# An empty VectorE instruction for the waits of a state-space scan, and TensorE sums of two units at a time

## The chip, the cores and the metric

The kernel runs on one core of one Trainium2 chip. The metric is the device time of one execution in microseconds (us). The engines named below are TensorE (PE in the profile, PEld for its weight loads), VectorE (DVE), ScalarE (ACT), GpSimd (POOL) and SyncE (SP, which issues most DMAs). Each engine works through its own instructions in order; between engines, and between an instruction and an earlier one of its own engine, order is kept by semaphores that an instruction waits for. A name such as DVEq is the instruction queue of that engine: a wait that is an instruction by itself is shown there as EVENT_SEMAPHORE.

## The reference

Two transformer-like layers on x of shape (4, 256, 512). Layer 0 is a latent attention plus a gated feed-forward part. Layer 1 adds a selective state-space block and a mixture of low-rank experts. All of the change lies in the state-space block, for each of the four batches with d = 1024 channels, n = 16 states and 256 time steps:

```python
xc = silu(causal_conv4(x) + conv_b)                # (d, t)
ssm_p = xc projected to 32 + 16 + 16               # dt_r, Bm, Cm, each rms-normed
dt = softplus(dt_r @ dt_proj + dt_bias)            # (d, t)
# scan over t, for each channel d and state n:
h = exp(dt_t * A) * h + dt_t * B_t * x_t
y = sum_n h * C_t
out = ((ys + D * xc) * silu(z)) @ out_proj
```

## The kernel before

Layer 0 comes first (up to about 330 us, with its last matmuls, L469, to 350 us). Then the scan runs through 128 units. Unit u works on batch b = u // 32 (a pass), on a chunk c = u % 32 // 4 of 128 channels, and on a group g = u % 4 of 4 states. A unit's tile has 128 partitions and 4 x 256 elements: partitions hold 32 channels for each of 4 states, and the free dimension holds 4 blocks of 32 channels by 256 time steps. The steps of a unit:

- `decays(u)` on ScalarE: four activations (L980) write the decay exp(dt * A) into one of three rotating tiles `decay`. A tile can be written again when the scan of three units before has read it.
- `scan_in(u)` on VectorE: the input product `bx` = B * (dt * x) (L986), from PSUM `brow` and the spread tile `dus`, into one PSUM tile of its own. As there is one such tile, the product waits for the scan of the unit before, which reads it.
- `scan(u)` on VectorE: one scan instruction over all 1024 elements (L1001), `h` = decay * h + bx. `h` has two buffers, so the scan must wait until the product of `h` and C of two units before has been made.
- the same function then makes `hc` = h * C on GpSimd (L1006; the last quarter of the last unit on VectorE). `hc` has three buffers.
- `states_sum(u)` on TensorE: four matmuls with a stacking matrix (L1018) add the 4 states into one quarter each of the PSUM tile `ysum`, as matmuls 32 columns wide. Each is traced as two, so that one unit has 8. In the first unit of a chunk (g = 0) a full-width matmul (L1016) opens the sum with D * xc; it waits until the sum of the chunk before has been copied out.
- After the fourth unit of a chunk, `take_sum` on ScalarE (L1023) copies the sum to `xc`, and `gate` on GpSimd (L1026) multiplies it by silu(z).

The order on every engine is written out by hand: the schedule is manual, and each engine executes its instructions in the order in which the main loop issues them. In iteration u the loop issues, in this order: `take_sum` where a chunk ended two units before; `decays(u + 2)`; the side work that is put at u (dictionary `at`); `scan_in(u)`; work put in the middle (`mid_at`); `scan(u)`; `gate`; late work; `states_sum(u - 1)`; work put at the end (`end_at`).

The side work prepares the next batch during the present pass. By its place in a pass of 32 units: norm and projection `px` (L757), convolution as matmuls (L804) with taps from ScalarE (L774, L779, L785) and additions on GpSimd (L811), in units 0 to 16; the silu of all of `xc` on ScalarE (L820, with a change of its function table) at unit 16; the projection `pp` (L831) in two halves, the first at the very end of unit 17, the second at 18; its squares and their mean (L837, L838) at 19; `nrm` on VectorE (L845) between product and scan of unit 21; then step sizes on TensorE (L870), ScalarE (L875 to L887) and GpSimd (L914 to L918, and `du`, L925), in units 21 to 30. `dt` and `du` go through DRAM (dtd, dud) and come back spread over the partitions (`dts`, `dus`) by DMAs from SP (L939). The experts' routing (L1053 to L1085) takes some 20 small VectorE instructions at unit 25 of passes 0 and 2. The output matmuls (L1114), the gate's input `pz` (L948) and the dense part (L1105) fill in.

A VectorE instruction carries one wait by itself; further ones stand in separate wait instructions in front of it, with up to two waits each. So before a scan there is one wait instruction, for the product and the decay, and the scan itself carries the wait for GpSimd.

Of the kernel before, what the change touches and what calls it, by code (L numbers as in the profile page):

```python
# [11 lines left out]
AF = mybir.ActivationFunctionType  # L12
# [16 lines left out]
NG = 4  # L29
# [12 lines left out]
def block_kernel(  # L42
# [24 lines left out]
    nc = tc.nc  # L67
# [51 lines left out]
    live = {}  # L119
# [363 lines left out]
    def go(gen, n=1000):  # L483
        for _ in range(n):
            if next(gen, 1) == 1:
                break
# [169 lines left out]
    xcs, nrms, dts, szs, crows = {}, {}, {}, {}, {}  # L656
# [15 lines left out]
    aneg = w1.tile([P, DC, NG, NU], F32, name="aneg")  # L672
# [15 lines left out]
        pads.append(t)  # L688

    decay = []  # L690

    def decay_tile(pool):
        t = pool.tile([P, NG, S], F32, name=f"decay{len(decay)}")
        nc.gpsimd.memset(t[:, :, 0:1], 0.0)
        decay.append(t)
# [268 lines left out]
    def lend(n, u):  # L964
        tag = lent[n][u]
        pool, bufs = (we, 3) if tag == "w_in" else (w1, 1)
        return pool.tile([P, NG, S], F32, tag=tag, name=n, bufs=bufs)

    def decays(u):
        b, c, g = u // PER, u % PER // NU, u % NU  # L970
        if u >= len(lent["d"]):
            da = decay[(u - 4) % 3]
        elif lent["d"][u] == "d":
            da = decay[0]
        else:
            da = lend("d", u)
            nc.gpsimd.memset(da[:, :, 0:1], 0.0)
        live["da", u] = da
        for k in range(NG):
            nc.scalar.activation(da[:, k, 1:], live["dts", b, c][:, k, 1:], AF.Exp,  # L980
                                 scale=aneg[:, c, k, g : g + 1])

    def scan_in(u):
        b, c, g = u // PER, u % PER // NU, u % NU
        bx = psx.tile([P, NG, S], F32, tag="bx", name="bx")
        nc.vector.tensor_tensor(  # L986
            bx, brow[g // 2][:, g % 2, :].unsqueeze(1).to_broadcast([P, NG, S]), live["dus", b, c], ALU.mult
        )
        live["bx"] = bx

    def scan(u, parts=1):
        b, c, g = u // PER, u % PER // NU, u % NU
        da, bx = live.pop(("da", u)), live["bx"]
        if u < len(lent["h"]):
            h, hc = lend("h", u), lend("hc", u)
        else:
            h = act.tile([P, NG, S], F32, tag="h", name="h", bufs=2)
            hc = act.tile([P, NG, S], F32, tag="hc", name="hc", bufs=3)
        for k in range(parts):
            n = slice(k * NG // parts, (k + 1) * NG // parts)  # L1000
            nc.vector.tensor_tensor_scan(  # L1001
                h[:, n].rearrange("p n t -> p (n t)"), da[:, n].rearrange("p n t -> p (n t)"),
                bx[:, n].rearrange("p n t -> p (n t)"), 0.0, ALU.mult, ALU.add,
            )

            (nc.vector if k == NG - 1 else nc.gpsimd).tensor_tensor(  # L1006
                hc[:, n], h[:, n],
                crows[b][:, g, :].unsqueeze(1).to_broadcast([P, NG // parts, S]), ALU.mult,
            )
        live["hc", u] = hc  # L1010

    def states_sum(u):
        b, c, g = u // PER, u % PER // NU, u % NU
        hc = live.pop(("hc", u))
        if g == 0:
            mm(ysum, lhsT=dgs[:, c, :], rhs=xcs[b][:, c, :], start=True, stop=False)  # L1016
        for k in range(NG):
            mm(ysum[k * NB : (k + 1) * NB, :], lhsT=stack, rhs=hc[:, k, :],  # L1018
               start=False, stop=(g == NU - 1))

    def take_sum(b, c):

        (nc.scalar.copy if b or c else nc.vector.tensor_copy)(xcs[b][:, c, :], ysum)  # L1023

    def gate(b, c):
        nc.gpsimd.tensor_tensor(  # L1026
            xcs[b][:, c, :], xcs[b][:, c, :], szs[b, c // 2][:, c % 2, :], ALU.mult
        )
# [84 lines left out]
    def out_mm(b, i, c):  # L1113
        mm(live["po", b, i], lhsT=xcs[b][:, c, i * P : (i + 1) * P], rhs=late_w["ow"][:, c, :],  # L1114
           start=False, stop=(c == DC - 1))
# [33 lines left out]
    for i in range(2):  # L1149
        v = vec[:, 6 + i, :]  # L1150
        nc.scalar.activation(px[:, i, :], px[:, i, :], AF.Identity, bias=v[:, V_CB : V_CB + 1],
                             scale=v[:, V_CW + KC - 1 : V_CW + KC])
# [33 lines left out]
    u, e, lw = live["u"], live["e"], live["lw"]  # L1186
# [21 lines left out]
    for n, t in (("dt", dt[:, 1, :]), ("du", du[:, 1, :])):  # L1208
        live[n, 0, 0] = scr.tile([2, P, S], F32, tag=n, name=f"{n}d")
        nc.sync.dma_start(live[n, 0, 0][1], t)  # L1210
    decays(0)
    scan_in(0)
    spread("dt", 0, 1)
    spread("du", 0, 1)
    b_rows(0, 1)
    c_rows(0, 1)
    decays(1)
    one_step(2)

    def open_act():  # L1220
        nonlocal act
        l0.close()
        act = ctx.enter_context(tc.tile_pool(name="act", bufs=1))
        decay_tile(act)
        decay_tile(act)
        for n, shape, d in (("rl", [P, HC, NE + P], rl_d), ("bw", [P, HC, D], base_d),
                            ("lb", [P, D], lb_d), ("ow", [P, DC, D], ow_d)):
            late_w[n] = act.tile(shape, F32, name=n), d
# [146 lines left out]
    total = B * PER  # L1375
    late, gated = [], []
    for u in range(total + 2):

        last = u - 2
        shut = (last // PER, last % PER // NU) if last >= 0 and last % NU == NU - 1 else None  # L1380
        if shut and shut != (0, 0) and u < total:
            take_sum(*shut)
        if 3 <= u < total - 2:
            decays(u + 2)
        for f, a in at.get(u, ()):
            f(*a)
        if u < total:
            if u:
                scan_in(u)
            for f, a in mid_at.get(u, ()):  # L1390
                f(*a)
        if shut == (0, 0):
            take_sum(0, 0)
        if u > total:
            b, c = shut
            for i in range(2):
                w = slice(i * P, (i + 1) * P)
                nc.vector.tensor_tensor(xcs[b][:, c, w], ysum[:, w], szs[b, c // 2][:, c % 2, w], ALU.mult)
        if u < total:
            scan(u, 1 if u < total - 1 else 4)  # L1400
            if u < 3:
                decays(u + 2)

        for g in range(2):
            o = u - NU - 1 - g
            if u < total and o >= 0 and o % NU == 0 and (o >= total - PER) == (g == 0):
                gate(o // PER, o % PER // NU)
                if g == 0:
                    gated.append(o % PER // NU)
        for f, a in late_at.get(u, ()):  # L1410
            f(*a)
        if 1 <= u <= total:
            states_sum(u - 1)
        if late and u >= total - PER + 22:
            c = late.pop(0)
            for i in range(2):
                out_mm(B - 1, i, c)
        for f, a in end_at.get(u, ()):
            f(*a)
        late, gated = late + gated, []  # L1420
        if u < 3:
            go(ff, (9, 12, 100)[u])
        if u == 2:
            open_act()
# [106 lines left out]
```

## Time and profile before

| | us |
|---|---|
| three timed runs | 839.10, 839.61, 840.86 |
| median of the runs | 839.61 |
| span of the profiled execution | 839.1 |
| VectorE busy | 655.1 (78%) |
| TensorE busy | 748.8 (89%) |
| ScalarE busy | 554.7 (66%) |
| GpSimd busy | 496.7 (59%) |
| products L986, 128 of 1.232 | 157.7 |
| scans L1001, 129 of 2.236 in the mean | 288.2 |
| hc L1006, 130 of 2.323 in the mean | 301.7 |
| sums L1018, 1024 traced matmuls | 89.6 |

The profiled execution has no time of its own beside its span; the span of 839.1 us equals the fastest of the three timed runs. A digit line of the page cuts the span into 40 slices, with the busy share in tenths. A timeline line has start, duration, engine, line, operation, written tile <- read tiles with their shapes, the number of merged instructions, and in brackets the idle time in front with what ended it. A table of busy times by stretch has, after the stretch and its length, the busy time (and instructions) of PE, PEld, DVE, ACT and POOL, the TensorE clock that was granted, the DMA share and GB/s.

### The profile page before, as it was taken

The numbers are of one execution on the slowest core, as the hardware profiler recorded it, in microseconds if no ns is written. First come the engines' busy times: TensorE is split into PE (matmuls) and PEld (weight loads), VectorE is DVE, ScalarE is ACT, GpSimd is POOL, SyncE is SP. The second block draws the span as 40 slices with busy tenths as digits, with TensorE's granted clock in tenths as the row PEclk, the third lists the DMA queues.
The fourth block names the chain that finished last, engine by engine and source line by source line (L and its number), as shares of the span: only waits on it lengthen the run. The fifth ranks groups of instructions, "written<-read, shape, count | busy, mean of one in ns | idle before, by whom it ended". The sixth has DMA issues, their size and how long they took to land.

```text
span 839.1 us, 11113 instructions
## 1 busy us (share of the span) xinstructions
PE 748.8 (89%) x3846; PEld 429.7 (51%) x3846; DVE 655.1 (78%) x604; ACT 554.7 (66%) x1124; POOL 496.7 (59%) x389
## 2 busy tenths in 40 slices
PE   4999999999999999999887899888999987956885
PEld 2665545666555676666543457444457444312331
DVE  4486756288634435798899999989999989999996
ACT  4335564435556277699896898687898786865561
POOL 3133332001343333688869799769699769798764
PEclk9799999999999999999999999989999989998998
DMA  7233332001222332554593554443553343343400
GB/s 226 63 101 105 97 101 62 1 1 38 76 76 80 114 57 64 151 140 125 137 215 114 150 155 125 110 103 117 144 164 114 88 113 111 103 125 102 113 26 25
DMA packets 68642, 86.71 MB, mean 103 GB/s; under 512 B 12221, under 2 KB 52169, under 8 KB 68458
## 3 DMA queue, kind: packets, MB, share of 16 engines
q1 hardware_dynamic: 58794, 65.81, 29.3%
q0 software_dynamic: 9072, 18.35, 7.9%
q10 hardware_dynamic: 720, 1.84, 0.6%
q8 instruction: 30, 0.49, 0.2%
q14 instruction: 26, 0.21, 0.1%
HBM read 66.58 MB, written 10.22 MB: 92 GB/s over the span
## 4 chain that ended last, share of the span: by engine, by line
PE 51%; DVE 25%; ACT 15%; POOL 5%; issue 3%; DMA 1%; DVEq 0%; POOLq 0%; ACTq 0%; SPq 0%
DVE h L1001 15%; ACT decay L980 7%; PE pg L444 6%; PE pu L444 5%; PE po L469 5%; PE px L757 4%; DVE bx L986 4%; POOL hc L1006 4%; PE av L397 4%; PE px L804 4%; PE ysum L1018 3%; PE scT L386 2%; DVE mpl L354 2%; PE pp L831 2%; PE po L1114 2%
## 5 line engine op out<-in xcount | busy, mean ns | idle before, releaser
L1006 POOL TENSOR_TENSOR hc<-h,cr 128x1024 f32<-128x1024 f32 (+1 forms) x130 | 301.7, 2323 | 79.9 <-DVE h L1001 67.5
L1001 DVE TENSOR_TENSOR_SCAN h<-decay,bx 128x1024 f32<-128x1024 f32 (+1 forms) x129 | 288.2, 2236 | 27.0 <-POOL hc L1006 4.7
L980 ACT ACTIVATE decay<-dts,aneg 128x255 f32<-128x255 f32 x504 | 213.4, 501 | 52.3 <-DVE h L1001 42.2
L986 DVE TENSOR_TENSOR bx<-brow,dus 128x1024 f32<-128x1024 f32 x128 | 157.7, 1232 | 5.0 <-DMA dus<-dud 0.6
L1018 PE MATMUL ysum<-hc,stack 128*32 128x256 f32 x1024 | 89.6, 419 | 42.2 <-POOL hc L1006 41.9
L456 POOL TENSOR_TENSOR hlo<-g,hhi 128x512 fp32r<-128x512 f32 x28 | 35.8, 1280 | 115.0 <-ACT hhi L455 115.0
L354 DVE TENSOR_REDUCE mpl<-sc 128x4 f32<-128x1024 f32 x64 | 76.7, 1219 | 22.8 <-PE sc L352 21.3
L427 POOL DMA_DIRECT2D wgu<-in_wgu x56 | 31.1, 555 | 95.9 <-PE pg L444 94.7
L388 ACT ACTIVATE pe<-scT 128x1024 f32<-128x1024 f32 x64 | 64.0, 1023 | 22.9 <-PE sc L352 14.3
L1114 PE MATMUL po<-ow,xc 128*128 128x512 f32 x128 | 69.4, 646 | 4.3 <-POOL xc L1026 3.9
L1018 PEld LDWEIGHTS ysum<-hc,stack 128*32 128x32 f32 x1024 | 21.3, 111 | 100.3 <-POOL hc L1006 70.6
L948 PE MATMUL pz<-xn1T,w_in 128*128 128x256 f32 x256 | 69.4, 420 | 0.0
L948 PEld LDWEIGHTS pz<-xn1T,w_in 128*128 128x128 f32 x256 | 50.8, 208 | 20.7 <-issue 11.9
L757 PE MATMUL px<-xn1T,w_in 128*128 128x256 f32 x256 | 60.9, 383 | 0.4 <-ACT sz L954 0.3
L757 PEld LDWEIGHTS px<-xn1T,w_in 128*128 128x128 f32 x256 | 47.6, 190 | 13.0 <-issue 2.5
L452 DVE SCALAR_TENSOR_TENSOR g<-g,pg 128x512 f32<-128x512 f32 x28 | 19.2, 686 | 43.1 <-ACT g L451 43.1
L444 PE MATMUL pg<-xhi,wgu 128*128 128x512 f32 x112 | 49.6, 443 | 1.0 <-ACT xhi L244 1.0
L469 PE MATMUL po<-wd,hhi 128*128 128x512 f32 x112 | 49.2, 439 | 0.0
L444 PE MATMUL pu<-xhi,wgu 128*128 128x512 f32 x112 | 47.6, 425 | 0.8 <-DVE g L454 0.8
L455 ACT CAST hhi<-g 128x512 fp32r<-128x512 f32 x28 | 17.3, 619 | 45.8 <-DVE g L454 45.8
L444 PE MATMUL pg<-xlo,wgu 128*128 128x512 f32 x112 | 44.9, 401 | 0.7 <-DVE xlo L251 0.7
L444 PE MATMUL pu<-xlo,wgu 128*128 128x512 f32 x112 | 44.5, 397 | 0.0
(237 smaller groups left out, 1276.8 us busy)
## 6 DMA issues: line engine op xcount, KB each, us to landing
dts<-dtd SPq DMA_DIRECT2D x124, 128.0 KB, 2.8
dus<-dud SPq DMA_DIRECT2D x124, 128.0 KB, 3.2
wgu<-in_wgu POOLq DMA_DIRECT2D x56, 256.0 KB, 2.7
w_in<-in_inz SPq DMA_DIRECT2D x16, 512.0 KB, 4.9
w_in<-in_inx SPq DMA_DIRECT2D x14, 512.0 KB, 4.3
dtd<-dt SPq DMA_DIRECT2D x15, 256.0 KB, 2.2
dud<-du SPq DMA_DIRECT2D x15, 256.0 KB, 2.2
wd<-in_wd POOLq DMA_DIRECT2D x7, 512.0 KB, 3.6
```

Source lines behind the costliest of these rows:

```text
L354: nc.vector.tensor_reduce(mpl2[b % 2][:, qb, 2 * hp : 2 * hp + 2, 16 + 2 * gq : 18 + 2 * gq], sc.rearrange("p i (f k) -> p i f k", f=2), A ...
L388: nc.scalar.activation(pes[b, k][:, 2 * t : 2 * t + 2, :], sc, AF.Exp)
L444: mm(ps, lhsT=wgus[i][:, hc, :], rhs=xs[j][:, hc, :], start=(hc == 0 and j == 0), stop=(hc == HC - 1 and j == 1))
L469: mm(po, lhsT=hids[th][j][:, m, i * P : (i + 1) * P], rhs=wd[:, m, :], start=False, stop=(m == MC - 1 and j == 1))
L757: mm(px[:, i, :], lhsT=w[:, i, hc, :], rhs=xns[b][:, hc, :], start=(hc == 0), stop=(hc == HC - 1))
L948: mm(pz[:, i, :], lhsT=w[:, i, hc, :], rhs=xns[b][:, hc, :], start=(hc == 0), stop=(hc == HC - 1))
L980: nc.scalar.activation(da[:, k, 1:], live["dts", b, c][:, k, 1:], AF.Exp, scale=aneg[:, c, k, g : g + 1])
L986: nc.vector.tensor_tensor(bx, brow[g // 2][:, g % 2, :].unsqueeze(1).to_broadcast([P, NG, S]), live["dus", b, c], ALU.mult)
L1001: nc.vector.tensor_tensor_scan(h[:, n].rearrange("p n t -> p (n t)"), da[:, n].rearrange("p n t -> p (n t)"), bx[:, n].rearrange("p n t -> ...
L1006: (nc.vector if k == NG - 1 else nc.gpsimd).tensor_tensor(hc[:, n], h[:, n], crows[b][:, g, :].unsqueeze(1).to_broadcast([P, NG // parts, ...
L1018: mm(ysum[k * NB : (k + 1) * NB, :], lhsT=stack, rhs=hc[:, k, :], start=False, stop=(g == NU - 1))
L1114: mm(live["po", b, i], lhsT=xcs[b][:, c, i * P : (i + 1) * P], rhs=late_w["ow"][:, c, :], start=False, stop=(c == DC - 1))
```

## The change

From unit 8 on, `scan_in` issues an empty VectorE instruction ahead of the product, and two dependencies are added to it by hand: on the last activation of the unit's own decay, and on the `hc` of two units before. As VectorE is in order, both hold for the scan too, so its own waits for ScalarE and GpSimd are left out when waits are assigned, and the scan keeps the one for the product. And `states_sum` is issued in even iterations only, for the units u - 2 and u - 1 one after the other.

```diff
+    made = {}
+    early = mybir.DependencyInfo(mybir.DependencyClass.Sync, mybir.DependencyReason.DATA)
...
         for k in range(NG):
-            nc.scalar.activation(da[:, k, 1:], live["dts", b, c][:, k, 1:], AF.Exp,
-                                 scale=aneg[:, c, k, g : g + 1])
+            made["da", u] = nc.scalar.activation(
+                da[:, k, 1:], live["dts", b, c][:, k, 1:], AF.Exp, scale=aneg[:, c, k, g : g + 1]
+            )
 
     def scan_in(u):
         b, c, g = u // PER, u % PER // NU, u % NU
+        if u >= 8:
+            i = nc.vector.engine_nop()
+            for n in (("da", u), ("hc", u - 2)):
+                tc.add_manual_dep(i.ins, made[n].ins.name, early, reason="the scan's waits")
         bx = psx.tile([P, NG, S], F32, tag="bx", name="bx")
...
-            (nc.vector if k == NG - 1 else nc.gpsimd).tensor_tensor(
+            made["hc", u] = (nc.vector if k == NG - 1 else nc.gpsimd).tensor_tensor(
                 hc[:, n], h[:, n],
...
-        if 1 <= u <= total:
+        if u and u % 2 == 0:
+            states_sum(u - 2)
             states_sum(u - 1)
```

In the built program VectorE has 120 empty instructions (L989) more, 116 of them with a wait instruction in front (for ScalarE), and 120 wait instructions less in front of the scans (12 for 132). The empty instruction itself carries the wait for GpSimd. The order of TensorE's matmuls changes by the sums alone. On SP, the first load of `w_in` for the gate waits for another buffer. On ScalarE and GpSimd the order stays; the first activation of many decays, and many hc's, get one more wait, for earlier work of their own engine.

## The prediction

> **What bounds the kernel now.** I read the digits of the page first, then a table of busy times for the four passes of the scan, then the timelines.
>
> ```profile
> PE   4999999999999999999887899888999987956885
> DVE  4486756288634435798899999989999989999996
> ACT  4335564435556277699896898687898786865561
> ```
>
> Up to 330 us TensorE is full, and the change touches none of that. From there VectorE is, and three others are close behind it. By pass (start:end, length, then PE, PEld, DVE, ACT, POOL busy):
>
> ```profile
> 364.40:465.60 101.20, 86.15 (x484) 53.91 (x483) 90.49 (x75) 86.12 (x195) 85.02 (x53) 0.95 0.60 152
> 465.60:588.70 123.10, 112.48 (x556) 61.32 (x554) 114.58 (x71) 102.41 (x232) 104.06 (x63) 0.92 0.46 124
> 588.70:712.80 124.10, 114.13 (x595) 63.97 (x595) 117.14 (x89) 102.03 (x234) 103.13 (x61) 0.95 0.44 121
> 712.80:828.40 115.60, 85.29 (x416) 33.50 (x415) 110.31 (x63) 71.62 (x153) 90.01 (x50) 0.94 0.31 86
> ```
>
> The last pass is VectorE's alone (110.3 of 115.6 us). In passes 0 to 2 ScalarE, GpSimd and TensorE have bursts that VectorE must wait for. VectorE's timeline shows a calm stretch, the burst of pass 0, and the stall of pass 1:
>
> ```profile
> ...
> 403.26 2.29 DVE L1001 TENSOR_TENSOR_SCAN h<-decay,bx 128x1024 f32<-128x1024 f32 x1 [0.69 <-POOL hc L1006]
> ...
> 419.37 0.48 DVE L845 SCALAR_TENSOR_TENSOR nrm<-pp,lnw,rs 64x256 f32<-64x256 f32 x1 [0.24 <-ACT rs L713]
> 419.77 2.27 DVE L1001 TENSOR_TENSOR_SCAN h<-decay,bx 128x1024 f32<-128x1024 f32 x1
> ...
> 545.65 0.48 DVE L845 SCALAR_TENSOR_TENSOR nrm<-pp,lnw,rs 64x256 f32<-64x256 f32 x1 [1.32 <-ACT rs L713]
> ...
> 603.53 1.23 DVE L986 TENSOR_TENSOR bx<-brow,dus 128x1024 f32<-128x1024 f32 x1
> 604.89 2.29 DVE L1001 TENSOR_TENSOR_SCAN h<-decay,bx 128x1024 f32<-128x1024 f32 x1
> 607.22 1.23 DVE L986 TENSOR_TENSOR bx<-brow,dus 128x1024 f32<-128x1024 f32 x1
> 608.58 2.29 DVE L1001 TENSOR_TENSOR_SCAN h<-decay,bx 128x1024 f32<-128x1024 f32 x1
> ```
>
> A unit takes 3.69 us: product 1.23, a gap of 0.13 (603.53 + 1.23 to 604.89), scan 2.29, a gap of 0.04. The gaps differ because the product waits for one thing, the scan before it, while the scan waits for three (product, decay, GpSimd's hc of two units before) and has a wait instruction of its own ahead of it, which takes 50 ns and cannot end before the product has. In pass 3:
>
> ```profile
> L1001 DVEq EVENT_SEMAPHORE  x31: 50/50/50, 714.1 to 824.7; - x31
> ```
>
> **The change, part by part.**
>
> *The gap.* In units 8 to 127 decay and hc are now waited for by an empty instruction (L989) ahead of the product, and the scan waits for the product alone, as the product waits for the scan. So its gap should be that of the product, 0.04 for 0.13. Rounded less, the two gaps are 132 and 35 ns: 120 units x 0.097 = 11.6 us. This is the whole gain if VectorE is never held by others.
>
> *The empty instruction.* Before has none on VectorE. The waits in front of the product (for dus, every fourth unit) begin as soon as the scan before has begun, and with them the product's gap stays 0.04; so the new wait for ScalarE should hide under the 2.29 us scan. The instruction itself I count as one that the engine executes. Below nothing is excluded: the product still waits for the scan's end. Above, I bound it by the shortest VectorE row, a memset of 128x1 (L87), 0.06 us; three of them start 0.03 apart. VectorE instructions without a wait begin 0.08 us before the one in front ends, so 0.06 fits in front of the scan's end. I take 0, and keep 120 x 0.06 = 7.1 us.
>
> [...]
>
> *What is queued behind the earlier waits.* Where decay or hc is late, the product now stands behind it too and 1.27 us (product and gap) that ran beside the lateness follow it. VectorE is in order, so `nrm` at units 21, 53 and 85, on which the next batch's steps depend, is held too. The hc of two units back normally ends 1.2 us before the product could start, so nothing is exposed; decay mostly ends earlier still. By unit, subtracting the ends in the traces: late ScalarE at 10 (0.7), 20, 51 (0.7), 58, 70 (0.7), 83 (0.4); late GpSimd at 13 to 19 (up to 4.4), 29 to 32 (0.6 falling), 43 to 48 (0.2), 61 to 64 (0.8 falling), 75 to 80 (0.2), 93 to 96 (0.6 falling). In pass 3 nothing.
>
> *The sums in pairs.* TensorE's timeline:
>
> ```profile
> 353.23 1.07 PE L1018 MATMUL ysum<-hc,stack 128*32 128x256 f32 x16
> 354.23 1.13 PE L870 MATMUL pdt<-nrm,dtw 32*128 32x256 f32 x4
> ...
> 411.88 5.35 PE L831 MATMUL pp<-xc,xpw 128*64 128x256 f32 x16 [3.91 <-ACT xc L820]
> 417.17 0.64 PE L1018 MATMUL ysum<-hc,stack 128*32 128x256 f32 x8
> ...
> 499.75 0.64 PE L1018 MATMUL ysum<-hc,stack 128*32 128x256 f32 x8
> 500.32 2.00 PE L804 MATMUL px<-pad,dg 128*128 128x256 f32 x8
> ...
> 534.82 0.70 PE L1016 MATMUL ysum<-xc,dgs 128*128 128x256 f32 x2 [3.07 <-ACT xc L1023]
> ```
>
> One sum takes 0.57 to the next start and 0.2 more at its borders with matmuls of another shape. Two in a row (353.23) take 1.00 and the same borders. A pair saves about 0.34. In the stretch 480 to 528, where TensorE never waited for a sum, 7 pairs give 2.4 us. And the matmul that opens a chunk (L1016) moves half the time a unit later: at 534.82 TensorE stood 3.07 us behind ScalarE's copy of the last chunk, with the projection `pp` (L831) queued behind; now `pp` goes first. So `pp` and `nrm` of pass 1 come several us earlier, and the 1.32 us stall at 545.65 goes. Pass 2 gains less there (0.66 of stall at 657.66).
>
> *The ring of three hc buffers.* The first sum of a pair now stands one slot later, so hc of unit u+3 may find its buffer unread. After unit 16 this bites: its sum, at 407.33 before, falls behind both halves of `pp`, which wait for ScalarE until 411.88 and end at 417.2. GpSimd's hc of unit 19 reads:
>
> ```profile
> 413.26 2.34 POOL L1006 TENSOR_TENSOR hc<-h,cr 128x1024 f32<-128x1024 f32 x1
> ```
>
> It would start at about 418.5 (417.2 + L1016 0.5 + sum 0.6 + 0.2) and end at 420.9. Unit 21's product waits for it: product to 422.1, `nrm` 0.5, scan at 422.65 instead of 419.77, +2.9 us. At unit 48 and 80 the earlier `pp` covers it.
>
> *Other queues.* SP: the first weight load of in_inz waits for a scan at 344.6 us instead of a sum at 336.3; behind it stand dtd, dud and the first spreads. Its matmuls ran at 349.68; a load takes 4.9 us, so 0 to 0.5 us, beside 0.3 saved by the first pair: taken as nothing. ScalarE and GpSimd get one more wait in about half the decays and hc's, on their own finished work: nothing while they are behind, 0.05 us when they wait for VectorE, which is not on the path then.
>
> *The sum* (position against before). Pass 0: +1.3 through the GpSimd burst (units 13 to 19), +2.9 at unit 21, replacing it, -1.0 over the ten units to 31, +1.0 at unit 29: +2.9. Pass 1: -1.9 over 19 units, -1.3 for the stall at `nrm`: -0.3; four units -0.4; units 58 to 61 about -0.1, since ScalarE's chain is two us earlier but the product is exposed; -0.3: -0.8 at 588.7. Pass 2: -3.1, ScalarE at 70 +0.9, GpSimd at 93 +0.8, small ones +0.3: -1.9. Pass 3: 32 x 0.097 = -3.1. Together -5.0. The profiled execution spans 839.1 us, 0.5 below the median of the runs, 839.61; I take the difference from the median: **834.6 us**.
>
> **The rivals.**
>
> *The empty instruction costs its place (slower).* If it starts only after the scan has ended and the product after it, a unit pays 0.06 (the memset) to 0.10 (a wait instruction and its hand-over). At 0.06: 834.6 + 7.1 = 841.7; it decides from 42 ns (5.0 / 120). For it: that a wait instruction on this queue costs 0.1. Against: short instructions start 0.03 apart, and next ones start before the end of the last. 0.2.
>
> *The hc ring or the early waits bite in every pass.* If passes 1 and 2 lose like pass 0 (2.9 each, ScalarE's bursts not coming earlier), 834.6 + 5.8 = 840.4, no change. For it: three passes with the same order around `pp`. Against: the 3.07 us stall that goes. 0.15.
>
> *The bursts move with VectorE.* If ScalarE's and GpSimd's work starts as much earlier as VectorE runs, nothing is exposed: 839.61 - 11.6 = 828.0, or 826.7 with the `nrm` stall. Against: ScalarE has no idle time from 367 to 403. 0.15.
>
> **How the numbers follow.** My forecast has 0.5. About 0.2% (1.7 us) is what can be told from no change. Faster: the forecast nearly whole (0.47) and the third rival (0.15): 0.62. The second rival gives most of "same", 0.12 with the forecast's edge; the first, and the second's bad half, 0.26 slower. The low end, 828.5, takes most of the third rival; the high end, 842.0, the first with its bound. The forecast's own range is 832 to 837.
>
> **What would show it.** Pass 3: units of 3.59 us with both gaps 0.04 (right), or 3.65 and more with a gap after the scan (first rival). Pass 0: hc of unit 19 released by the sum. Pass 1: no stall before `nrm`, L1016 behind `pp`. VectorE's idle time should read "POOL hc" and "ACT decay" in front of the product instead of the scan. It is wrong if pass 3 isn't about 3 us shorter, or if passes 0 to 2 lose more than pass 3 gains.

## The result, and the profile after

| | us |
|---|---|
| before, median of 22 runs | 839.38 |
| after, median of 22 runs | 840.49 |
| ratio after / before, 95% interval | 1.0015 [1.0007, 1.0023] |
| span of the profiled execution, before / after | 839.1 / 840.1 |

In this set the change makes the kernel slower by 0.15%. A second set of runs of the same program gave 840.69 us, where before took 840.81 (ratio 0.9995 [0.9982, 1.0009]), so no clear difference is left. I had forecast 834.6 us, a clear gain. The time lies in the range given, but the gain did not come. A run's time is about 1.8 us longer than the span of its core (841.86 for 840.1 in the profile after), so the profile of before, with 839.1, belongs to a run of about 840.9, the slowest of the three listed and not the fastest; the forecast, a difference taken from the median, does not hang on that.

The digits of the page after:

```profile
PE   4999999999999999989796989988899997976885
DVE  4486755288734435887789999998999999999997
ACT  4335564435556276689886788877898786865661
```

Up to the 17th slice VectorE's digits are nearly those of before. The next four, which hold most of pass 0, read 8 7 7 8 for 9 8 8 9: VectorE waits more there. In the rest, 9s stand for 8s in two slices, and an 8 for a 9 in one. The four passes in the profile after, read as before from the product of unit 8 on (start:end, length, busy PE, PEld, DVE, ACT, POOL, granted clock, DMA share, GB/s):

```profile
364.05:471.61 107.56, 90.23 (x504) 59.17 (x496) 90.41 (x75) 86.12 (x195) 85.44 (x53) 0.92 0.60 146
471.61:594.05 122.44, 108.87 (x564) 62.17 (x564) 114.44 (x71) 102.36 (x232) 104.31 (x63) 0.93 0.46 125
594.05:716.38 122.33, 109.85 (x590) 65.83 (x589) 117.09 (x88) 101.64 (x234) 102.75 (x62) 0.94 0.43 122
716.38:829.40 113.02, 86.46 (x414) 36.83 (x414) 110.30 (x63) 71.25 (x153) 89.56 (x49) 0.88 0.32 87
```

VectorE's busy time is that of before in every pass (90.4, 114.4, 117.1, 110.3 for 90.5, 114.6, 117.1, 110.3). Pass 0 is 6.4 us longer, the others 0.7, 1.8 and 2.6 shorter. So the gain of the gap is there, and something else takes it away. VectorE's timeline after shows both:

```profile
...
549.58 0.47 DVE L847 SCALAR_TENSOR_TENSOR nrm<-pp,lnw,rs 64x256 f32<-64x256 f32 x1
549.98 2.27 DVE L1008 TENSOR_TENSOR_SCAN h<-decay,bx 128x1024 f32<-128x1024 f32 x1
...
564.34 1.23 DVE L993 TENSOR_TENSOR bx<-brow,dus 128x1024 f32<-128x1024 f32 x1 [1.33 <-POOL hc L1013]
565.61 2.29 DVE L1008 TENSOR_TENSOR_SCAN h<-decay,bx 128x1024 f32<-128x1024 f32 x1
570.05 1.23 DVE L993 TENSOR_TENSOR bx<-brow,dus 128x1024 f32<-128x1024 f32 x1 [2.16 <-ACT decay L982]
...
581.60 1.23 DVE L993 TENSOR_TENSOR bx<-brow,dus 128x1024 f32<-128x1024 f32 x1 [0.83 <-POOL hc L1013]
...
608.47 1.23 DVE L993 TENSOR_TENSOR bx<-brow,dus 128x1024 f32<-128x1024 f32 x1
609.74 2.29 DVE L1008 TENSOR_TENSOR_SCAN h<-decay,bx 128x1024 f32<-128x1024 f32 x1
612.06 1.23 DVE L993 TENSOR_TENSOR bx<-brow,dus 128x1024 f32<-128x1024 f32 x1
```

Calm units take 3.59 us with both gaps at 0.035 (608.47 + 1.23 to 609.74, and 609.74 + 2.29 to 612.06). The stall in front of `nrm` in pass 1 is gone. But units 57, 58 and 61 stand in front of their product for 1.33, 2.16 and 0.83 us, and the product runs only when the wait is over. In the groups this is the idle time that moved from the scan (27.0 us before) to the product (5.0 before):

```profile
L1008 DVE TENSOR_TENSOR_SCAN h<-decay,bx 128x1024 f32<-128x1024 f32 (+1 forms) x129 | 288.1, 2236 | 8.1 <-PE po L469 3.2
...
L993 DVE TENSOR_TENSOR bx<-brow,dus 128x1024 f32<-128x1024 f32 x128 | 157.6, 1232 | 27.8 <-POOL hc L1013 12.0
```

Before, 1.23 us of product lay beside each such wait; after, they follow it. The instructions that do the waiting take 13 and 21 ns in the median, and the calm gaps are 0.035 us with them (count, durations min/median/max in ns, first and last start):

```profile
L989 DVEq ENGINE_NOP  x120: 5/13/15, 363.9 to 828.0; - x120
L989 DVEq EVENT_SEMAPHORE  x116: 21/21/21, 363.2 to 825.8; - x116
```

TensorE's timeline at the turn from convolution to projection in pass 1 is as forecast, L1023 (the L1016 of before) now behind both halves of `pp`:

```profile
537.33 1.94 PE L833 MATMUL pp<-xc,xpw 128*64 128x256 f32 x8 [1.24 <-ACT xc L822]
...
540.25 1.94 PE L833 MATMUL pp<-xc,xpw 128*64 128x256 f32 x8
542.12 0.70 PE L1023 MATMUL ysum<-xc,dgs 128*128 128x256 f32 x2
```

GpSimd's timeline in pass 0 has four waits for a sum (in front of hc of units 7, 9, 11 and 19), where before has none. The longest are 3.39 us in front of hc of unit 9 and 5.86 us in front of those of units 19 and 20:

```profile
374.76 2.36 POOL L1013 TENSOR_TENSOR hc<-h,cr 128x1024 f32<-128x1024 f32 x1 [3.39 <-PE ysum L1025]
...
422.22 4.67 POOL L1013 TENSOR_TENSOR hc<-h,cr 128x1024 f32<-128x1024 f32 x2 [5.86 <-PE ysum L1025]
```

It happens in pass 1 as well. hc of unit 55 waits 2.91 us for a sum and ends at 564.30, and this is what unit 57's product waits for, which starts at 564.34:

```profile
561.93 2.37 POOL L1013 TENSOR_TENSOR hc<-h,cr 128x1024 f32<-128x1024 f32 x1 [2.91 <-PE ysum L1025]
```

### The profile page after: what moved, and what is told of

Its sections match the earlier page's. It is cut to its first block, busy times and chain, and to the rows that moved or that the text cites. A ratio compares the mean times of both kernels' runs of the same rounds, so it can differ in the third digit from the quotient of the medians.

```text
span 840.1 us, 11287 instructions
## 1 busy us (share of the span) xinstructions
PE 743.8 (89%) x3846; PEld 439.8 (52%) x3846; DVE 655.1 (78%) x604; ACT 553.9 (66%) x1124; POOL 496.5 (59%) x389
## 3 DMA queue, kind: packets, MB, share of 16 engines
q10 hardware_dynamic: 720, 1.84, 0.6%
## 4 chain that ended last, share of the span: by engine, by line
PE 47%; DVE 26%; ACT 12%; POOL 8%; issue 4%; DMA 2%; SPq 0%; ACTq 0%; DVEq 0%; POOLq 0%
DVE h L1008 12%; DVE bx L993 7%; PE pg L444 6%; POOL hc L1013 6%; PE pu L444 5%; PE po L469 5%; PE av L397 4%; PE px L759 4%; ACT decay L982 3%; PE scT L386 2%; PE px L806 2%; PE ysum L1025 2%; DVE mpl L354 2%; PE po L1121 2%; PE po L464 2%
## 5 line engine op out<-in xcount | busy, mean ns | idle before, releaser
L993 DVE TENSOR_TENSOR bx<-brow,dus 128x1024 f32<-128x1024 f32 x128 | 157.6, 1232 | 27.8 <-POOL hc L1013 12.0
L1025 PE MATMUL ysum<-hc,stack 128*32 128x256 f32 x1024 | 80.6, 416 | 41.6 <-POOL hc L1013 41.6
L1025 PEld LDWEIGHTS ysum<-hc,stack 128*32 128x32 f32 x1024 | 25.4, 113 | 90.1 <-POOL hc L1013 62.4
```

What stands on the lines that cost most here:

```text
L993: nc.vector.tensor_tensor(bx, brow[g // 2][:, g % 2, :].unsqueeze(1).to_broadcast([P, NG, S]), live["dus", b, c], ALU.mult)
```

## The experiments

For each kernel the table has the median, its ratio to before on the same chip with the 95% interval, and from the profile what each pass loses (+) or gains (-). For that I take the start of a scan less its start in the profile of before, set to zero at unit 1, since layer 0, which nothing here touches, differs by up to 2 us between profiles. The passes are read at units 32, 64, 96 and 127.

| kernel | us | ratio | pass 0 | 1 | 2 | 3 | sum |
|---|---|---|---|---|---|---|---|
| changed | 840.49 | 1.0015 [1.0007, 1.0023] | +5.9 | -0.7 | -1.8 | -2.6 | +0.9 |
| changed_again | 840.69 | 0.9995 [0.9982, 1.0009] | +5.8 | -0.6 | -1.7 | -2.6 | +1.0 |
| single_sums | 840.71 | 1.0010 [0.9995, 1.0025] | +0.7 | +1.6 | -0.6 | -2.6 | -0.9 |
| pairs_only | 840.04 | 1.0001 [0.9986, 1.0016] | +4.0 | -3.0 | -1.1 | 0.0 | -0.1 |
| empty_no_waits | 840.01 | 1.0001 [0.9986, 1.0016] | -0.3 | -0.3 | 0.0 | +0.4 | -0.2 |
| pairs_from_32 | 835.02 | 0.9929 [0.9910, 0.9949] | +3.4 | -2.2 | -0.6 | -1.6 | -1.0 |
| pairs_32_again | 834.71 | 0.9943 [0.9930, 0.9956] | +0.7 | -3.2 | -0.8 | -2.6 | -5.9 |
| pairs_32_no_empty | 835.34 | 0.9931 [0.9913, 0.9948] | 0.0 | -3.0 | -1.1 | 0.0 | -4.1 |
| pairs_32_empty_96 | 833.78 | 0.9913 [0.9890, 0.9936] | 0.0 | -3.0 | -0.8 | -2.6 | -6.4 |
| pairs_32_empty_calm | 833.17 | 0.9905 [0.9884, 0.9926] | -0.4 | -1.9 | -1.9 | -2.9 | -7.0 |
| empty_behind | 831.27 | 0.9887 [0.9864, 0.9909] | +3.5 | -5.6 | -4.0 | -3.0 | -9.1 |
| behind_pairs_32 | 826.02 | 0.9834 [0.9810, 0.9858] | -1.3 | -6.4 | -2.8 | -3.0 | -13.5 |
| single_behind | 833.98 | 0.9934 [0.9917, 0.9950] | -1.4 | -0.4 | -1.7 | -2.5 | -6.0 |
| sum16_single | 837.93 | 0.9975 [0.9961, 0.9988] | +4.6 | -1.3 | -1.7 | -2.6 | -1.0 |
| first_sums_single | 840.62 | 1.0003 [0.9990, 1.0016] | +5.5 | -0.5 | -1.7 | -2.6 | +0.8 |
| pairs_from_12 | 838.98 | 0.9992 [0.9980, 1.0004] | +5.2 | -2.5 | -1.6 | -2.6 | -1.4 |
| hc_in_front | 841.06 | 1.0007 [0.9993, 1.0020] | 0.0 | +0.8 | +0.7 | -0.9 | +0.5 |

The profile of pairs_from_32 is of its slowest execution, 838.17 us; the five others took 832.81 to 835.40. The reason comes below.

### The two parts apart

Theory A blamed the pairs in pass 0, theory B the early waits.

single_sums, against the changed kernel:

```diff
-        if u and u % 2 == 0:
-            states_sum(u - 2)
+        if 1 <= u <= total:
             states_sum(u - 1)
```

> The changed kernel with the sums one unit at a time again; the empty instruction stays. Theory A (sums in pairs come too late for the ring of three hc buffers in pass 0): hc of unit 9 starts within 2.5 us of its scan's start, no idle time of GpSimd ended by ysum at 370 to 385 us, pass 0 ends about 1 us later than before instead of 5.9, and the kernel takes about 835.5 us, 4 below before. Theory B (the early waits themselves cost pass 0 its time): pass 0 still ends 5 us or more later, 840 to 841 us.

pairs_only leaves the empty instruction and its two dependencies out:

```diff
-        if u >= 8:
-            i = nc.vector.engine_nop()
-            for n in (("da", u), ("hc", u - 2)):
-                tc.add_manual_dep(i.ins, made[n].ins.name, early, reason="the scan's waits")
```

> The changed kernel without the empty instruction: waits as before, only the sums in pairs. Theory A: hc of unit 9 waits 3 us for ysum, pass 0 ends 3 to 5 us later than before, pass 1 gives back 1 to 2 at nrm, the gap in front of the scan stays 0.13; 841 to 843 us, slower than before. Theory B: nothing lost in pass 0, 837 to 838.5 us.

pairs_from_32 has the empty instruction, and pairs after pass 0 only:

```diff
-        if u and u % 2 == 0:
+        if u <= 32:
+            if u:
+                states_sum(u - 1)
+        elif u % 2 == 0:
             states_sum(u - 2)
             states_sum(u - 1)
```

> Empty instruction throughout, sums one at a time in pass 0 and in pairs from unit 32 on. Theory A: pass 0 as with single sums (+1 us), passes 1 to 3 as in the changed kernel (-0.7, -1.8, -2.6, together -5): about 835.5 us, and at or below the kernel with single sums. Theory B: as the changed kernel, 840 us or more.

Pass 0 went as theory A had it: +0.7 with single sums, +4.0 with pairs alone. With pairs alone GpSimd waits for the same sum as in the changed kernel:

```profile
372.39 2.37 POOL L1009 TENSOR_TENSOR hc<-h,cr 128x1024 f32<-128x1024 f32 x1 [2.73 <-PE ysum L1021]
```

But theory A had forgotten the other passes. Pairs alone gave back 3.0 and 1.1 us in passes 1 and 2, more than was expected, and took 840.04 us and not 841 to 843. Single sums took 840.71 and not 835.5. Their largest loss in pass 1 is at unit 58 (2.5 us by the starts of the scans), where the product stands 4.24 us behind ScalarE. In before the scan stood there for 1.72 us, its product done. The first line is of before:

```profile
566.05 2.29 DVE L1001 TENSOR_TENSOR_SCAN h<-decay,bx 128x1024 f32<-128x1024 f32 x1 [1.72 <-ACT decay L980]
```

```profile
565.77 1.23 DVE L993 TENSOR_TENSOR bx<-brow,dus 128x1024 f32<-128x1024 f32 x1 [4.24 <-ACT decay L982]
```

So pass 0 was not B's (with single sums it ends at +0.7, not at 5 or more), but early waits of the kind that B had in mind cost time in pass 1. Neither part alone gains, for different reasons; with pairs from unit 32 on, where they do no harm, the kernel gains 0.7%.

### The empty instruction by itself

empty_no_waits has single sums and keeps the instruction, without the two dependencies:

```diff
             i = nc.vector.engine_nop()
-            for n in (("da", u), ("hc", u - 2)):
-                tc.add_manual_dep(i.ins, made[n].ins.name, early, reason="the scan's waits")
```

> Single sums, and an empty VectorE instruction that waits for nothing in front of 120 products; the scan keeps its own wait instruction. If the empty instruction is free: the time of before, 839.4 us within 0.4, and gaps of 0.035 and 0.13 us as before. If it costs the 0.06 us of the shortest VectorE row: 846.6.

It costs nothing that the interval of some 1.3 us either way shows, about 10 ns for each of the 120. The gap in front of the scan stays 0.13 us (133 ns in the median of pass 3; 728.91 + 1.23 to 730.28 in rounded numbers), that behind it 0.03:

```profile
726.59 2.29 DVE L1006 TENSOR_TENSOR_SCAN h<-decay,bx 128x1024 f32<-128x1024 f32 x1
728.91 1.23 DVE L991 TENSOR_TENSOR bx<-brow,dus 128x1024 f32<-128x1024 f32 x1
730.28 2.29 DVE L1006 TENSOR_TENSOR_SCAN h<-decay,bx 128x1024 f32<-128x1024 f32 x1
```

hc_in_front, with single sums too, asks what makes the 0.13. The empty instruction waits for hc alone, so that the wait instruction in front of the scan holds one wait, for the product, instead of two:

```diff
-            for n in (("da", u), ("hc", u - 2)):
+            for n in (("hc", u - 2),):
```

> Sums one at a time, the empty instruction in front of the product waits for hc alone; the scan then has a wait instruction for the product alone and carries the wait for ScalarE. If any wait instruction that waits for the product costs the 0.097 us: gaps of 0.13 us in front of the scan as before, no gain, 840 us or more. If it is the second wait in that instruction that costs: gaps of 0.035 us, and pass 3 is 3 us shorter.

The gap was neither: 0.10 us (103 ns in the median of pass 3; 732.27 + 1.23 to 733.61 in rounded numbers), and the wait instruction takes 21 ns for the 50 of before. The first line is from the row of the scan's line in pass 3, the others from the timeline:

```profile
L1008 DVEq EVENT_SEMAPHORE  x31: 21/21/21, 718.8 to 828.6; - x31
```

```profile
732.27 1.23 DVE L993 TENSOR_TENSOR bx<-brow,dus 128x1024 f32<-128x1024 f32 x1
733.61 2.29 DVE L1008 TENSOR_TENSOR_SCAN h<-decay,bx 128x1024 f32<-128x1024 f32 x1
```

So of the 0.097 us that the change saves per calm unit, 0.03 is the second wait (0.133 for 0.103) and 0.07 the wait instruction as such (0.103 for 0.035), where what it waits for is the instruction just in front.

### Pairs and empty instruction where they are known to do no harm

pairs_32_no_empty is pairs_from_32 without the empty instruction, so the edits of pairs_only and pairs_from_32 together.

> Waits as before (no empty instruction), sums one at a time in pass 0, in pairs from unit 32 on. Theory A (the pairs lose only in pass 0; later they take away the stalls in front of nrm at unit 53, of the scan at 58 and of the routing at 89): 1.4 + 1.6 + 1.1 us gained, about 835.3 us. Theory B (pairs win nothing by themselves, the 0.7% of the kernel with pairs from 32 on needs both parts): 839 us.

835.34 us was measured. Pass 0 is that of before to 0.02 us, and the gains are where they were expected: 1.42 at `nrm` of unit 53, 1.58 at unit 58, 1.09 at unit 89. The kernel with the empty instruction in front of the product took 835.02 and 834.71, so there it adds nothing that can be told. Unit 58's scan stands right behind its product:

```profile
543.24 0.47 DVE L847 SCALAR_TENSOR_TENSOR nrm<-pp,lnw,rs 64x256 f32<-64x256 f32 x1
...
560.68 1.23 DVE L989 TENSOR_TENSOR bx<-brow,dus 128x1024 f32<-128x1024 f32 x1
562.04 2.29 DVE L1004 TENSOR_TENSOR_SCAN h<-decay,bx 128x1024 f32<-128x1024 f32 x1
```

pairs_32_empty_96 has the empty instruction in pass 3:

```diff
-        if u >= 8:
+        if u >= 96:
```

> The same, and the empty instruction in pass 3 alone (units 96 to 127). Theory A: 2.6 to 3.0 us less than without it, since the gap of 0.097 us goes in 31 units and at most one of them is late: about 832.5 us. Theory B: the gap of pass 3 is not worth its sum, less than 1 us.

833.78, which is 1.6 us less, with intervals that overlap. By the profile pass 3 gains 2.6 us, and unit 96 loses 0.27 to a late hc.

pairs_32_empty_calm leaves the empty instruction out in the 15 places of passes 0 to 2 that showed a wait, and in unit 102 of pass 3:

```diff
+        v = u % PER
-        if u >= 8:
+        if u >= 8 and (u >= 3 * PER and v != 6 or v not in (6, 10, 11, 12, 13, 14, 15, 16, 17, 19, 20, 25, 26, 28, 29)):
```

> Pairs from unit 32 on, and the empty instruction in the 75 units in which the product of the kernel with it waited for no late decay and no late hc. Theory A (the early wait costs the product's 1.27 us wherever decay or hc is late, and nothing elsewhere): below both kernels, 830 to 832 us, and at least 3 us below the kernel with the empty instruction everywhere from unit 8. Theory B (VectorE's gain is taken back by the next burst in passes 0 to 2): the time of the kernel with the empty instruction in pass 3 alone, 832.5 us.

833.17, 0.6 us below the last one, which the intervals do not tell apart; 830 to 832 was theory A's. In pass 1 both theories hold in part: 0.9 us are gained up to unit 52, but the scan of unit 58 then waits 1.84 us for ScalarE's decay, and unit 62, which was not in the list, waits 1.18 us in front of its product, for GpSimd's hc (the wait for the decay was over at 574.2 us; hc of unit 60 ended at 577.5, and the product started at 577.58). Choosing units chases the waits from one to the next.

### The empty instruction behind the product

If the trouble is that the product stands behind the waits, the waits can stand behind the product. empty_behind moves the same three lines from `scan_in` to the start of `scan`; pairs as in the changed kernel:

```diff
     def scan_in(u):
-        if u >= 8:
-            i = nc.vector.engine_nop()
...
     def scan(u, parts=1):
...
+        if u >= 8:
+            i = nc.vector.engine_nop()
+            for n in (("da", u), ("hc", u - 2)):
+                tc.add_manual_dep(i.ins, made[n].ins.name, early, reason="the scan's waits")
         for k in range(parts):
             nc.vector.tensor_tensor_scan(
```

> The changed kernel with the empty instruction moved from in front of the product to between product and scan; sums in pairs throughout. Theory A (the wait instruction holds the scan by 0.097 us only because it waits for the product; with the scan alone waiting for the product, waits for ScalarE and GpSimd that stand behind the product are done while it runs): gaps of 0.035 us as in the changed kernel, and the product of a unit with late decay or hc runs beside the lateness again: 836 to 838 us. Theory B (an instruction between product and scan can't begin before the product's end): gap in front of the scan back at 0.1 us or more, the time of the kernel with pairs alone, 840 us.

831.27 us, below what theory A had: 9 us less than the changed kernel, from the place of one instruction. The gaps stay 0.035, and a late decay costs what is left of it behind the product:

```profile
562.52 1.23 DVE L989 TENSOR_TENSOR bx<-brow,dus 128x1024 f32<-128x1024 f32 x1
564.35 2.29 DVE L1008 TENSOR_TENSOR_SCAN h<-decay,bx 128x1024 f32<-128x1024 f32 x1 [0.60 <-ACT decay L982]
```

The profiles of the two kernels have the long stretches of TensorE's half clock (more on them below) at the same places in passes 0 and 1: 10.2 us from 357, 6.8 from 412, 10.2 from 552. The one difference, a stretch from 583 that lasts 6.8 us in the changed kernel and 3.4 here, falls away in changed_again, which has 3.4 too and the same shifts. So they can be compared pass by pass: in front costs 2.4, 4.9, 2.2 and 0.5 us more than behind, 10.0 together.

behind_pairs_32 is the same with the edit of pairs_from_32 on top, single sums in pass 0.

> The same with sums one at a time in pass 0 and pairs from unit 32 on. Theory A: pass 0 ends 0 to 1 us earlier than before, pass 3 gives 3.0, passes 1 and 2 4.1 and 1 to 2 more: 829 to 831 us, below the kernel with the empty instruction in calm units (833.2). Theory B: 835.3 us, as without the empty instruction.

826.02 us, 1.7% below before and the fastest of all. Passes 1 to 3 in its profile:

```profile
463.21:579.93 116.72, 105.02 (x568) 61.02 (x563) 114.46 (x70) 102.00 (x232) 104.03 (x63) 0.99 0.49 131
579.93:701.24 121.31, 111.14 (x589) 65.88 (x588) 117.19 (x88) 101.62 (x233) 103.01 (x61) 0.93 0.46 124
701.24:813.80 112.56, 88.30 (x417) 38.63 (x416) 110.30 (x64) 71.26 (x153) 90.48 (x50) 0.86 0.33 89
```

Pass 1 has 114.46 us of VectorE in 116.72, against 123.10 before. single_behind has the edit of single_sums on top instead.

> Sums one at a time throughout, the empty instruction between product and scan. If empty instruction and pairs add up: pairs from 32 on are worth 5 us and the two together 14, so 9 are left, about 831 us; the same program with the empty instruction in front of the product took 840.7. If the stalls at units 53, 58 and 89 that the pairs remove take VectorE's gain back: 834 to 836 us.

833.98: the rival reading was right, and the parts do not add up but help each other. Without pairs, `nrm` of pass 1 stands 3.15 us behind ScalarE and the scan of unit 58 2.44 us, and pass 1 gains 0.4 instead of 6.4.

```profile
543.03 0.48 DVE L847 SCALAR_TENSOR_TENSOR nrm<-pp,lnw,rs 64x256 f32<-64x256 f32 x1 [3.15 <-ACT rs L715]
...
560.10 1.23 DVE L989 TENSOR_TENSOR bx<-brow,dus 128x1024 f32<-128x1024 f32 x1
563.77 2.29 DVE L1008 TENSOR_TENSOR_SCAN h<-decay,bx 128x1024 f32<-128x1024 f32 x1 [2.44 <-ACT decay L982]
```

### Pass 0: the ring, and the clock

sum16_single keeps the pairs but for the sums of units 16 and 17:

```diff
-        if u and u % 2 == 0:
+        if u in (17, 18):
+            states_sum(u - 1)
+        elif u and u % 2 == 0:
```

> The changed kernel with the sums of units 16 and 17 one at a time, so that the sum of 16 stands in front of both halves of pp. Theory A (ring of three hc buffers): hc of unit 19 follows its scan instead of ysum, the 1.6 us which the changed kernel loses between units 20 and 21 stay away, 839 us. Rival (nrm waits for pp through ScalarE in any case): the 1.6 us stay, 840.6 us.

837.93. hc of unit 19 follows its scan (413.88, beside 422.22 in the changed kernel), and the step between units 20 and 21 is gone: -0.3 for +1.6. `nrm` does not stand there, so the rival reading, that the 1.6 us stay, falls. But VectorE comes there later than in the changed kernel, having lost 2.6 us at unit 20 instead of 1.0. The next hc still waits, 5.22 us, but isn't needed as early:

```profile
413.88 2.35 POOL L1013 TENSOR_TENSOR hc<-h,cr 128x1024 f32<-128x1024 f32 x1 [0.58 <-DVE h L1008]
421.45 2.38 POOL L1013 TENSOR_TENSOR hc<-h,cr 128x1024 f32<-128x1024 f32 x1 [5.22 <-PE pr L1044]
```

What this is worth in time is not clear from it: at the end of pass 0 the kernel stands 1.3 us better than the changed one, but 1.1 of that was there at unit 14, before the edit acts. The two programs are the same up to unit 16. What differs is the clock. In every profile TensorE falls to half clock between 355 and 358 us, and by rows of 1 us it has stood idle for 1.7 us or more of the 4 us before (the expectations call the stretch at half clock a pulse). It comes back after 3.4 us in before and single_sums, after 6.8 in sum16_single, and after 10.2 in the changed kernel; up to unit 14 they have lost 1.6 (single_sums), 3.1 and 4.2 us. Theory C: the stretch falls on a TensorE that is the bottleneck of units 7 to 12, and its length costs the rest. changed_again was the same program once more.

> The changed kernel once more, for another profile of it and for its clock. Theory C (a pulse of half clock on TensorE at 357 us, which lasts 3.4 or 10.2 us from run to run, falls on the bottleneck of units 7 to 12): the shift of pass 0 is +3 us where the pulse is short, +6 us where it is long; the mean clock over the runs is 0.94 to 0.95, below the 0.95 to 0.96 of the kernels with single sums; 840.5 us. Against C: +6 us with a short pulse.

The long stretch came again, and with it +5.8: it agrees with C but could not tell. first_sums_single tried to remove the cause:

```diff
-        if u and u % 2 == 0:
+        if 1 <= u <= 4:
+            states_sum(u - 1)
+        elif u and u % 2 == 0:
```

> The changed kernel with the sums of units 0 to 3 one at a time, so that TensorE's work from 340 to 357 us is that of before. Theory C (the pulse of half clock at 357 us costs 2.7 us of pass 0): if the pulse is 3.4 us long, pass 0 ends 3 us later than before and the kernel takes 838 us; if it stays at 10.2, the pairs after unit 4 make it long, pass 0 ends 6 us later, 840.6 us. Against C: short pulse and still +6 us.

It stayed at 10.2 us and the loss at +5.5: undecided again. Then pairs_32_again showed the cost in one program, since pairs_from_32 had met a long stretch:

> The kernel with the empty instruction from unit 8 and pairs from unit 32 once more. Its first profile had a pulse of 10.2 us at 357 us, a shift of +3.4 us at the end of pass 0 and 838.2 us, while its other runs took 832.8 to 835.4. Theory C: with a pulse of 3.4 us this profile shows +0.7 us at the end of pass 0, as with single sums, and a total 2.5 to 3 us lower. Against C: +3.4 us with a short pulse.

This time it was 3.4 us, and pass 0 lost 0.7 instead of 3.4: one program, 2.7 us apart, with 6.8 us more of half clock in this stretch. The whole difference is there at unit 16, before the next stretch begins. It is one pair of profiles. First the profile of pairs_from_32, then that of pairs_32_again (after length and busy times the granted clock, third from the end):

```profile
357.00:360.40 3.40, 2.52 (x13) 1.20 (x12) 3.23 (x3) 3.40 (x9) 2.08 (x2) 0.51 0.44 127
360.40:363.80 3.40, 3.40 (x15) 1.67 (x14) 3.37 (x2) 3.40 (x10) 2.68 (x3) 0.50 0.94 255
363.80:367.20 3.40, 3.40 (x15) 1.67 (x14) 3.33 (x3) 3.34 (x6) 2.15 (x2) 0.50 0.78 159
```

```profile
357.00:360.40 3.40, 3.40 (x18) 1.67 (x16) 3.23 (x3) 3.40 (x10) 2.08 (x2) 0.52 0.09 26
360.40:363.80 3.40, 3.35 (x24) 2.26 (x20) 3.27 (x2) 3.40 (x10) 2.90 (x2) 0.98 0.86 237
363.80:367.20 3.40, 3.40 (x22) 2.44 (x21) 3.33 (x3) 3.37 (x8) 2.37 (x1) 1.00 1.01 243
```

pairs_from_12 keeps the pairs out of that stretch, and has them in the rest of pass 0:

```diff
-        if u and u % 2 == 0:
+        if u <= 12:
+            if u:
+                states_sum(u - 1)
+        elif u % 2 == 0:
```

> The changed kernel with the sums of units 0 to 11 one at a time and pairs after that. Theory C: the pulse at 357 us is 3.4 us long, unit 13 stands at +1.4 us as with single sums instead of +3.9, the ring still costs 1.6 us at unit 21, pass 0 ends at +3 us, and the kernel takes about 838 us. Against C (the pairs of units 4 to 11 don't matter and the ring is all): pass 0 ends at +5 us or more, 840.5 us.

The stretch was 3.4 us, and unit 13 stood at +1.4 as with single sums: up to there theory C is right. But pass 0 still ended at +5.2. The scans of units 20 and 21 each lose over 2 us, the first behind ScalarE's chain, which is 2.2 us later than with single sums at the copy of chunk 3 (408.02 for 404.60, less the 1.2 us by which this profile is later at unit 1), the second behind hc of unit 19, in the ring. In the first line the profile names a DMA, but the wait instruction for ScalarE's decay, at 417.62, is what held the queue:

```profile
417.91 1.23 DVE L993 TENSOR_TENSOR bx<-brow,dus 128x1024 f32<-128x1024 f32 x1 [4.02 <-DMA dts<-dtd]
...
423.87 1.23 DVE L993 TENSOR_TENSOR bx<-brow,dus 128x1024 f32<-128x1024 f32 x1 [2.40 <-POOL hc L1013]
```

This profile and that of sum16_single both have a further stretch of half clock, 3.4 us at 394 or 395, and both stand 4.0 us in front of unit 20's product; the changed kernel, without it, stands 2.33 us there. So the end of pass 0 holds two causes, the clock and the ring, and a VectorE that is already late from the one feels less of the other. Their shares in the changed kernel's +5.9 are not shown. There are estimates for each alone: 2.7 for the clock by one program's two profiles, 1.6 for the ring by the step that goes with it.

## Why the prediction was wrong

**The gap: right.** 0.035 for 0.132 us, and in pass 3 -2.6 us where I had -3.1; most of the rest is unit 102, whose decay was 0.44 us late.

**The empty instruction: right at 0.** It takes 5 to 15 ns (13 in the median) on the queue and moves nothing that shows (empty_no_waits, ratio 1.0001 [0.9986, 1.0016]). The first rival falls.

**What is queued behind the earlier waits: the step that failed.** I had listed most of the right units (not 11, 12, 57 and 102), but priced most by the lateness that the trace of before showed, and units 58 to 61 at "about -0.1, since ScalarE's chain is two us earlier but the product is exposed". ScalarE was that much earlier: unit 58's decay came at 570.05 us for 566.05 before, in a pass that began 5.9 us later. The product still stood 2.16 us behind it and ran only then. In the changed kernel units 57 to 63 lose 1.6 us where the gaps alone would gain 0.7; with the instruction behind the product they gain 2.0. Before that, up to unit 52, pass 1 gains 0.5 us in front and 1.8 behind, where I had 1.9. By pass (0 to 3) the instruction behind the product gives +3.5, -5.6, -4.0 and -3.0 us, in front of it +5.9, -0.7, -1.8 and -2.6; forecast were +2.9, -3.7, -1.1 and -3.1. Over all four passes the place costs 10.0 us, about as much as the 11.6 us of gap are worth. The fault, as I read it, was in the arithmetic of a burst: a faster VectorE arrives earlier at a ScalarE or GpSimd that isn't faster, so the lateness there grows with the gaps saved since the last burst, and then the product is exposed too. Unit 43 fits that, with 0.63 us behind an hc that I had put at 0.2, but no run tests this arithmetic by itself.

**The sums in pairs: right in kind, more than forecast in passes 1 and 2, less in pass 0.** The stall at `nrm` went (-1.4 for -1.3). I had not seen that the stalls at unit 58 (1.58) and in front of the routing at 89 (1.09) go with the pairs as well; pairs_32_no_empty shows both without any empty instruction.

**The ring: right in its place, too small.** hc of unit 19 was released by the sum, at 422.2 us for my 418.5; the step to unit 21 is the 1.6 us that I had. But the same ring already bites at unit 9, and again at unit 55 in pass 1, which I had not listed. In before hc of unit 9 followed its scan without a gap.

**The clock: not in the sum at all.** I took TensorE's pace from a profile with 3.4 us of half clock from 358 us; the changed kernel has 10.2 there in both profiles. In the pair of profiles of one program the longer stretch went with 2.7 us, close to the 3.0 by which pass 0 missed the forecast of +2.9. That it is worth as much in the changed kernel isn't shown: pairs_from_12 met the short stretch and still ended pass 0 at +5.2.

**The sum itself.** The terms of pass 1, -0.3 - 0.4 - 0.1 - 0.3, make -1.1 and not the -0.8 that I carried on, so by its own terms the forecast is 834.3 us. That changes nothing in the account above.

**The rivals.** The second, that early waits or ring bite in every pass (840.4), came closest, and I gave it 0.15. Its early waits did bite in passes 0 to 2; its ring in pass 0, and in pass 1 at one unit (57). What I had against it, the 3.07 us that TensorE no longer waits in front of L1023, happened, but it pays TensorE's chain and not the exposed products. The third, bursts that move with VectorE, falls with the 27.8 us of waits in front of products.

## What to carry to other kernels

Where an in-order engine's wait instruction stands right behind the instruction it waits for, give that wait to the next real instruction, and let an empty one carry the waits for other engines (here the gap in front of the scan went from 0.132 to 0.035 us): but put it behind the last work that doesn't need them. In front, the lateness of others held the product too (27.8 us of idle time in front of products, for 5.0 before); here the place alone was 840.5 against 831.3 us. And price a saving on the bounding engine from its next wait for others: time saved in front of a burst can be lost again in it, unless the burst's own chain gets shorter too. Here pass 1 gained 0.4 us without the pairs and 6.4 with them.

## What I had not expected of the hardware

TensorE's granted clock in these profiles is 1.0 or 0.5, and the half-clock stretches in the scan are 3.4, 6.8 or 10.2 us long. At 355 to 358 us it was 10.2 in five of the six profiles of kernels that sum in pairs there (6.8 in the other), and 3.4 in eleven of the twelve others. In the first of the rows above, from 357.0 to 360.4 us, TensorE was busy 2.52 of 3.40 us in pairs_from_32, where the stretch went on, and 3.40 in pairs_32_again, where it ended. But the two rows after that have it busy throughout in pairs_from_32 too, at half clock, so what ends a stretch isn't shown. In the same 3.40 us it was busy 1.54 in the changed kernel and 3.08 in before. That pairs bunch its work, leave it idle there and so meet the long stretch is a guess of mine: no run here moved that idle time alone.
